# Two soft layers and an attention share their memory, and the turn from dispatch to combination is cut into five stages

## The chip, the cores and the metric

The kernel runs on one core of a Trainium2 chip. The metric is the device time of one execution in microseconds (us). A core has five engines that work at the same time, each from its own queue in order: TensorE (PE in the profile, with PEld for its weight loads), VectorE (DVE), ScalarE (ACT), GpSimd (POOL) and SyncE (SP), which here only issues DMAs; ACT and POOL issue some as well. TensorE writes to PSUM; the other tiles lie in SBUF.

## The reference

The input `x` is 4 x 1024 tokens of width 128, 4,096 tokens in all. Six layers run one after the other, each on a layer norm of `x`: a mixture of experts (MoE), a Mamba layer, the MoE again, a soft mixture of experts ("soft a"), a gated linear attention, and the soft mixture again ("soft b"). The change touches the last three and the constants of the attention.

The soft layer computes `logits = x phi^T + phi_b` for 2,048 slots (64 experts of 32 slots). `D` is its softmax over the 32 slots of an expert; `C` is its softmax over the 64 experts. Then

```
X_tilde = einsum('tznp,tzd->npd', D, x)          # dispatch: 2,048 slot rows
X_tilde = tanh(layernorm(clip(X_tilde)))
Y_tilde = einsum('npd,ndH->npH', X_tilde, expert_w) + expert_b
Y       = einsum('tznp,npH->tzH', C, Y_tilde)    # combination
x       = x + 0.5 * Y
```

The attention has 16 heads of 8. From x it makes q and k (with silu), v, a forget gate f and an output gate g (sigmoids of low-rank products). Its state obeys `S = f * S + k v^T`, its output is `o = q . S`; `o * g` is divided by its root mean square per head, weighted, multiplied by `Wo` and added to x.

## The kernel before

Tokens lie in 32 tiles of 128; `x` stays in SBUF all the time. Inside each layer the order of the instructions on every engine is written out by hand: the program order of the Python code is the queue order.

**Soft layer, `soft_bounded` (L1169).** One loop over k covers two stages. In dispatch, k counts 64 half tiles (128 tokens x 1,024 slots). `logits(k)` makes two products in a PSUM tile of pool `psl` (two buffers), VectorE takes the row's minimum of the negated logits (`nmh`), `expo(k)` exponentiates on ScalarE, `total(k)` sums each expert's 32 slots and inverts on VectorE, `weigh(k)` multiplies on GpSimd, and `spread(k)`, three steps later, adds into the four accumulators `px` in PSUM. From k = 64, u = k - 64 counts 64 units of combination: eight blocks t of 512 tokens, eight pairs c of slot chunks. `clogits(u)` makes two transposed logits tiles, `cexpo(u)` exponentiates them into `L` (pool `lp`, 14 buffers) and adds them on GpSimd into `acc`; after the eighth pair a GpSimd addition folds `acc` to one tile. `denom(t)`, at u = 8t + 9, sums `acc` over the partitions on TensorE (`pd`, L1364) and VectorE inverts it (`rd`). `cweigh(u)` ten units later multiplies L by `rd` on VectorE, `mix(u)` twelve units later multiplies by `yt` on TensorE into `py`. `finish(t)` transposes and adds into x, then calls `after`, which makes the next layer's norm statistics.

**The turn** lies between: at u = 3 to 8 each of the four quarters of `px` goes through `mid_a` (clip on VectorE, transposes on TensorE, statistics on VectorE, a root by POOL's power), one unit later `mid_b` (tanh on ScalarE, transposes, copy), one unit later `mid_c` (32 small matmuls with the experts' weights, bias into `yt`). `maxima(j0, n)` (L1266) reduces `nmh` to one value a token, transposes it on TensorE, and SP brings it by two DMAs through DRAM to the last row of `xT`, which the combination reads. It is called for tiles 0 to 27 at k = 60 and for tiles 28 to 31 at u = 0. All other PSUM tiles of the soft layer come from one pool `psm` of four buffers.

**Attention, `gla_layer` (L1723).** It opens its own pools, loads its weights by ScalarE's DMA queue, builds constants (`sel`, `spread_w`, `hsel`, `hback`) on GpSimd, VectorE and TensorE, and then runs 32 steps: eight half sequences of 512 tokens, four steps each. A step k holds `spread(k+1)` (v's rows copied over partitions, TensorE), `scan(k)` (VectorE), `times_q(k)` (GpSimd), `times_k(k+1)` (VectorE) and `sums(k-2)` (TensorE). `prologue(u)` makes q, k, v, f, g of a half in four pieces, one a step, in the four steps before the half; `epilogue(u)` normalises and adds into x in five pieces, from two steps after the half.

The three layers follow each other as whole calls: `soft("a")`, `gla_layer`, `ln_root`, `soft("b")`, each with pools of its own that reuse the memory of the one before. Soft b sets the rows from 96 on of its `xT` to 1 on GpSimd (L1193) and computes `smod` again. All of this is inside a branch on a flag that bounds the logits; the other branch uses `soft_layer`.

**Second MoE, `moe_experts(..., "b")`.** 16 blocks on TensorE; its hook `extra` issues one piece a block, here the loads of the soft layers' expert weights on ScalarE's queue (`arrive`).

Of the kernel before, what the change touches and what calls it, by code (L numbers as in the profile page):

```python
# [18 lines left out]
P = 128  # L19
# [52 lines left out]
def macaron_kernel(ctx: ExitStack, tc: tile.TileContext, a: dict, out: bass.AP):  # L72
# [1096 lines left out]
    def soft_bounded(phiN, phiM, pbc, ew, eb, tag, ln, first=None, rest=None, after=None, last=False):  # L1169
# [12 lines left out]
        with ExitStack() as s:  # L1182
            sp = s.enter_context(tc.tile_pool(name=f"soft{tag}", bufs=1))
            xnp = s.enter_context(tc.tile_pool(name=f"sxn{tag}", bufs=3))
            ep = s.enter_context(tc.tile_pool(name=f"sep{tag}", bufs=3))
            dp = s.enter_context(tc.tile_pool(name=f"sdp{tag}", bufs=4))
            lp = s.enter_context(tc.tile_pool(name=f"slp{tag}", bufs=14))
            wk = s.enter_context(tc.tile_pool(name=f"swk{tag}", bufs=4))
            psl = s.enter_context(tc.tile_pool(name=f"spl{tag}", bufs=2, space=PSUM))
            psm = s.enter_context(tc.tile_pool(name=f"spm{tag}", bufs=4, space=PSUM))  # L1190

            xT = sp.tile([P, T], F32, name="xT")
            (nc.vector if first else nc.gpsimd).memset(xT[96:P, :], 1.0)  # L1193
            yt = sp.tile([P, NSC, D], F32, name="yt")

            nmh = sp.tile([P, NT, 2], F32, name="nmh")
            nm = sp.tile([P, NT], F32, name="nm")
            nm_d = dram.tile([1, T], F32, name=f"nm_d{tag}")
            smod = group_sum(sp)


            xns, pts, ls, exs, sms, dms, px = {}, {}, {}, {}, {}, {}, {}

            def norm(j):
                g, i = divmod(j, 4)
                if i == 0:
                    xns[g] = xnp.tile([P, 4, D], F32, name="xn")
                ln_apply(xns[g][:, i, :], j, ln)

            def turn(g):  # L1210
                pts[g] = psl.tile([P, HS], F32, name="pt", tag="l")
                for i in range(4):
                    nc.tensor.transpose(
                        pts[g][:, i * P : (i + 1) * P], xns[g][:, i, :], ident
                    )
# [37 lines left out]
            def spread(k):  # L1253
                j, hf = divmod(k, 2)
                dmf = dms.pop(k).rearrange("p n s -> p (n s)")
                for q in range(2):
                    if j == 0:
                        px[hf * 2 + q] = psm.tile([P, 512], F32, name="px", tag="m")
# [881 lines left out]
```

## Time and profile before

| | |
|---|---|
| three executions | 2184.3, 2188.48, 2188.88 us, median 2188.48 |
| profiled execution | 2190.58 us, its span 2188.8 us |
| mean granted TensorE clock | 0.933 |
| second MoE's matmuls | 849 to 971 us of the span |
| soft a, dispatch | 993.5 (first logits) to 1235.7 |
| soft a, combination | 1237.1 (first `clogits`) to 1502 (last update of x) |
| attention, scans | 1516.2 to 1672.6 |
| soft b, dispatch | 1691.8 (first logits) to 1922.4 |
| soft b, combination | 1923.7 to 2184.9 |

Times in the profile count from the start of the span. A line of the timeline begins with start and duration, then engine, source line, operation, output<-input and shapes; a bracket at its end gives how long the engine had been idle before it and what ended that idle time. A float32 product of 128 x 128 by 128 x 512 appears as two MATMUL records; four records in a row are one `clogits`, half a `logits` step with `spread`, or one `mix`. Records of matmuls overlap, so that the distance between their weight loads is the better measure of pace.

### The profile page before, as it was taken

To read this page: it belongs to the slowest core of one execution; us is meant where nothing else is said; L and a number is where in the kernel's file an instruction comes from. 1 tells how busy PE (TensorE), PEld (TensorE's weight loads), DVE (VectorE), ACT (ScalarE), POOL (GpSimd) and SP (SyncE) were. 2 spreads that over 40 slices of the span, in tenths; PEclk is the share of its full clock that TensorE was granted. 3 is DMA by queue.
4 is the path that set the end of the run, shared out by engine and by line. 5 is a ranking of instruction groups with operands and counts; after the bars stand their busy time and mean duration, and the time that the engine had idled before them with its cause. 6 is when DMAs were issued, how large, how long until landed. Compare 5 with 4: busy or idle time off the path is not lost. (4 is left out here: it accounts for less than half of the span.)

```text
span 2188.8 us, 17956 instructions
## 1 busy us (share of the span) xinstructions
PE 1895.3 (87%) x5893; PEld 882.4 (40%) x5893; DVE 1408.3 (64%) x1840; ACT 949.5 (43%) x1593; POOL 1388.7 (63%) x897
## 2 busy tenths in 40 slices
PE   5798488888989866977999899998888999989998
PEld 3465223333333324752444344443233344434443
DVE  6221579878788883126889655556976888744445
ACT  4232465667766523323444333333542333343331
POOL 2677378888988956516886566662533555556663
PEclk9998789999999886998999999998977999999999
DMA  6211522323332321520000000000000000000000
GB/s 233 87 51 49 158 89 97 120 103 101 126 106 99 120 93 50 142 72 25 19 19 7 1 1 0 1 0 6 0 0 1 1 0 0 1 1 6 10 10 16
DMA packets 65117, 110.70 MB, mean 51 GB/s; under 512 B 8159, under 2 KB 41583, under 8 KB 60149
## 3 DMA queue, kind: packets, MB, share of 16 engines
q1 hardware_dynamic: 53990, 87.10, 11.8%
q0 software_dynamic: 8192, 16.79, 2.9%
q10 hardware_dynamic: 2834, 5.59, 0.9%
q8 instruction: 48, 0.79, 0.1%
q14 instruction: 53, 0.43, 0.1%
HBM read 90.00 MB, written 19.44 MB: 50 GB/s over the span
## 5 line engine op out<-in xcount | busy, mean ns | idle before, releaser
L1248 POOL TENSOR_TENSOR dm<-ex,sm 128x1024 f32<-128x1024 f32 x128 | 246.4, 1926 | 166.1 <-DVE sm L1244 95.4
L980 POOL TENSOR_TENSOR hc<-hst,Cs 128x1024 f32<-128x1024 f32 x127 | 281.1, 2222 | 57.2 <-DVE hst L963 33.0
L1356 POOL TENSOR_TENSOR acc<-acc,L 128x1024 f32<-128x1024 f32 x96 | 225.8, 2353 | 113.5 <-ACT L L1348 112.8
L995 PE MATMUL py<-hc,ident 128*128 128x512 f32 x512 | 273.6, 663 | 27.3 <-POOL hc L980 27.1
L1348 ACT ACTIVATE L<-pl,pbc 128x512 f32<-128x512 f32 x256 | 161.9, 683 | 281.1 <-PE pl L1338 270.6
L1236 ACT ACTIVATE ex<-l,nmh 128x1024 f32<-128x1024 f32 x128 | 142.7, 1115 | 293.4 <-DVE nmh L1231 290.8
L1227 PE MATMUL l<-phiT,xT 128*128 128x512 f32 x512 | 248.6, 610 | 12.3 <-ACT ex L1236 9.1
L1259 PE MATMUL px<-dm,xn 128*128 128x512 f32 x512 | 243.3, 598 | 2.5 <-POOL dm L1248 2.2
L1338 PE MATMUL pl<-xT,phiM 128*128 128x512 f32 x512 | 242.8, 599 | 0.0
L1382 PE MATMUL py<-L,yt 128*128 128x512 f32 x512 | 238.4, 593 | 4.4 <-DVE L L1372 4.4
L1231 DVE TENSOR_REDUCE nmh<-l 128x1 f32<-128x1024 f32 x128 | 155.4, 1214 | 76.4 <-PE l L1227 76.0
L953 ACT ACTIVATE dA<-delta,A 128x512 f32<-128x512 f32 x256 | 177.3, 720 | 50.9 <-DVE hst L963 46.2
L945 POOL TENSOR_TENSOR dBu<-du,Bs 128x1024 f32<-128x1024 f32 x78 | 171.4, 2198 | 6.5 <-ACT dA L953 5.4
L450 ACT ACTIVATE hT<-ph,cols 128x512 f32<-128x512 f32 x128 | 87.9, 687 | 190.7 <-PE ph L446 186.3
L995 PEld LDWEIGHTS py<-hc,ident 128*128 128x128 f32 x512 | 94.1, 198 | 171.5 <-issue 115.8
L963 DVE TENSOR_TENSOR_SCAN hst<-dA,carry,dBu 128x512 f32<-128x512 f32 x128 | 155.3, 1262 | 11.8 <-ACT dA L953 6.3
L963 DVE TENSOR_TENSOR_SCAN hst<-dA,dBu 128x512 f32<-128x512 f32 x128 | 147.4, 1202 | 16.9 <-POOL dBu L945 8.5
L1227 PEld LDWEIGHTS l<-phiT,xT 128*128 128x128 f32 x512 | 98.1, 195 | 145.4 <-issue 115.6
L1243 DVE TENSOR_REDUCE sm<-ex 128x32 f32<-128x1024 f32 x128 | 154.5, 1207 | 0.0
L465 DVE TENSOR_TENSOR eo<-po,b 128x512 f32<-128x512 f32 x32 | 22.1, 691 | 196.3 <-PE po L460 188.7
L1382 PEld LDWEIGHTS py<-L,yt 128*128 128x128 f32 x512 | 96.8, 190 | 127.3 <-issue 117.0
L1372 DVE TENSOR_TENSOR L<-L,rd 128x1024 f32<-128x1024 f32 x128 | 147.0, 1210 | 0.1
(292 smaller groups left out, 2967.9 us busy)
## 6 DMA issues: line engine op xcount, KB each, us to landing
Cs<-bc_d SPq DMA_DIRECT2D x32, 1024.0 KB, 6.1
Bs<-bc_d SPq DMA_DIRECT2D x78, 256.0 KB, 3.0
w<-in_w SPq DMA_DIRECT2D x4, 2048.0 KB
y_d<-zero SPq DMA_DIRECT2D x1, 4096.0 KB
y<-y_d SPq DMA_DIRECT2D x16, 256.0 KB, 4.2
ys_d<-eo SPq DMA_DIRECT2D x16, 256.0 KB
ew<-in_ew ACTq DMA_DIRECT2D x12, 320.0 KB, 3.1
x<-in_x SPq DMA_DIRECT2D x8, 256.0 KB, 5.7
```

The costliest lines, as they stand in the source:

```text
L945: eng.tensor_tensor(dBu, r["du"], r.pop(("B", n)).unsqueeze(2).to_broadcast([P, HB, NC]), ALU.mult,)
L953: nc.scalar.activation(dA, r["delta"][:, :, c], AF.Exp, scale=A[:, c * DS + n : c * DS + n + 1],)
L963: nc.vector.tensor_tensor_scan(hst[:, :, c], r.pop(("dA", n, c)), dBu[:, :, c], 0.0 if h == 0 else carry[b][:, c, n : n + 1], ALU.mult, AL ...
L980: eng.tensor_tensor(hc, r.pop(("h", n)), Cs.unsqueeze(2).to_broadcast([P, HB, NC]), ALU.mult)
L995: nc.tensor.matmul(r["py"][:, c, :], ident, hc[:, :, c], start=False, stop=(n == DS - 1))
L1227: nc.tensor.matmul(l[:, q * 512 : (q + 1) * 512], xT[:, j * P : (j + 1) * P], phiN[:, o : o + 512], start=True, stop=True,)
L1248: nc.gpsimd.tensor_tensor(dms[k], exs.pop(k), sms.pop(k).unsqueeze(2).to_broadcast([P, NG, PS]), ALU.mult,)
L1259: nc.tensor.matmul(px[hf * 2 + q], xns[j // 4][:, j % 4, :], dmf[:, q * 512 : (q + 1) * 512], start=(j == 0), stop=(j == NT - 1),)
L1338: nc.tensor.matmul(pl[:, i, :], phiM[:, (2 * c + i) * P : (2 * c + i + 1) * P], xT[:, t * TB : (t + 1) * TB], start=True, stop=True,)
L1348: nc.scalar.activation(L[:, i, :], pl[:, i, :], AF.Exp, bias=pbc[:, 2 * c + i : 2 * c + i + 1], scale=-1.0,)
L1356: nc.gpsimd.tensor_tensor(accs[t], accs[t], L, ALU.add)
L1382: nc.tensor.matmul(pys[t], yt[:, 2 * c + i, :], L[:, i, :], start=(c + i == 0), stop=(c == CS - 1 and i == 1),)
```

## The change

1. **The turn.** `mid_a` and `mid_b` are each split: clip; transposes and statistics; tanh; transposes and copy; experts' matmuls. The five stages stand one unit apart, so the turn takes u = 3 to 10.
2. **Maxima.** `maxima` becomes a generator of two parts: the reduction, and a step later the transpose, the copy and the DMAs. The first call's parts stand at k = 59 and 60, the second's at u = 10 and 11.
3. **Last block's sums.** For t = 7 GpSimd adds only the pairs 0 to 6 and folds; TensorE adds the last pair's two tiles itself in `pd`. The reciprocal is then done in two halves, each followed by the weighing of half of the block's first L; `cweigh` of that unit is dropped.
4. **Shared memory.** `soft_shared` opens `xT`, `nmh`, `nm`, the pools `sxn`, `sep`, `slp`, and PSUM `psl` (two), `psA` (two), `psB` (two) once for soft a, attention and soft b. The attention keeps q, k, v, f, g, the transposed input and the low-rank product of even halves in columns of `xT`, those of odd halves in a small pool of its own; its states and `og` are `L` tiles, its `qs` are `ex` tiles.
5. **Joints.** The attention's first prologue, first `spread` and `times_k` (`begin`) run in the units of soft a after the last `clogits`. Soft a's last `finish` runs at the attention's step 1. Soft b's first norm, turn and two logits (`opening`) run at the attention's steps 30 to 33, and the attention's last epilogue at steps 1 to 4 of soft b's loop. The rows of ones are set in three memsets on GpSimd at steps 28 and 30.
6. **Constants.** The attention's weight loads and constants, and `smod`, are made piece by piece in the second MoE's `extra`, some on VectorE in place of GpSimd.

```diff
+    def soft_shared(s, smod):
...
+        sp = pool("soft", 1)
+        m = SimpleNamespace(
+            xT=sp.tile([P, T], F32, name="xT"),
+            nmh=sp.tile([P, NT, 2], F32, name="nmh"),
+            nm=sp.tile([P, NT], F32, name="nm"),
+            smod=smod,
+            xnp=pool("sxn", 3), ep=pool("sep", 3), lp=pool("slp", 14),
+            psl=pool("spl", 2, space=PSUM),
+            psA=pool("spa", 2, space=PSUM), psB=pool("spb", 2, space=PSUM),
+        )
+        def four(odd, shape, name):
+            return (m.psB if odd % 2 else m.psA).tile(shape, F32, name=name, tag="m")
...
+        def maxima(j0, n):
+            js = slice(j0, j0 + n)
+            nc.vector.tensor_reduce(nm[:, js], nmh[:, js, :], AX.X, ALU.min)
+            yield
+            pt = psl.tile([P, HS], F32, name="pt", tag="l")
+            nc.tensor.transpose(pt[:n, :P], nm[:, js], ident)
...
-            elif c > 1:
+            elif c > 1 and not (t == NB - 1 and c == CS - 1):
                 nc.gpsimd.tensor_tensor(accs[t], accs[t], L, ALU.add)
-            if c == CS - 1:
+            if c == CS - 1 - (t == NB - 1):
...
         def denom(t):
+            pd = m.four(1, [P, TB], "pd")
+            parts = [accs.pop(t)]
+            if t == NB - 1:
+                L = Ls[t * CS + CS - 1]
+                parts += [L[:, 0, :], L[:, 1, :]]
+            for i, part in enumerate(parts):
+                nc.tensor.matmul(
+                    pd, smod.rearrange("p g s -> p (g s)"), part,
+                    start=(i == 0), stop=(i == len(parts) - 1),
+                )
+            rds[t] = m.four(t, [P, TB], "rd")
+            if t < NB - 1:
+                nc.vector.reciprocal(rds[t], pd)
+                return
+            for h in range(2):
+                hs = slice(h * TB // 2, (h + 1) * TB // 2)
+                nc.vector.reciprocal(rds[t][:, hs], pd[:, hs])
+                L = Ls[t * CS]
+                nc.vector.tensor_tensor(
+                    L[:, :, hs], L[:, :, hs],
+                    rds[t][:, hs].unsqueeze(1).to_broadcast([P, 2, TB // 2]), ALU.mult,
+                )
...
+        def opening():
+            for i in range(4):
+                norm(i)
+            yield
+            turn(0)
+            take(0)
+            yield
+            for k in range(2):
+                logits(k)
+                expo(k)
+                yield
...
+            for k in range(NK + CS * NB + XL):
+                next(others, None)
+                if k > 0:
+                    next(before, None)
...
-                        if not new and r == 4:
-                            maxima(0, NT - 4)
-                    if u == 0:
-                        maxima(NT - 4, 4)
+                    if not new and r == 3:
+                        rows = maxima(0, NT - 4)
+                if u == 10:
+                    rows = maxima(NT - 4, 4)
+                if r in (3, 4) and k >= NK - 8 or u in (10, 11):
+                    next(rows, None)
                 if u >= SEAM:
                     v = u - SEAM
-                        for f, o in ((mid_a, 0), (mid_b, 1), (mid_c, 2)):
+                    for f, o in ((mid_a, 0), (mid_a2, 1), (mid_b, 2), (mid_b2, 3), (mid_c, 4)):
...
+                    if u >= CS * NB:
+                        next(tail, None)
...
+        def view(c, n, rows=P):
+            v = m.xT[:rows, c * HB : (c + n) * HB]
+            return v.rearrange("p (i t) -> p i t", t=HB) if n > 1 else v
...
+            qkv = r["qkv"] = own.bp.tile([P, 3, HB], F32, name="qkv") if odd else view(0, 3)
+            fg = r["fg"] = own.bp.tile([P, 2, HB], F32, name="fg") if odd else view(3, 2)
...
+        def begin():
+            yield from prologue(0, lambda name: large(name)[:, 0, :])
+            spread(0)
+            times_k(0)
+            yield
...
+            one.body(tail=begin)
+            run(begin)
+            opening = two.opening()
+            hooks = {k: [lambda: next(opening)] for k in (-2, -1, 0, 1)}
+            hooks[gla.first + 1] = [one.finish]
+            gate = slice(*gla.gates)
+            hooks[-4] = [
+                lambda: nc.gpsimd.memset(m.xT[96:P, : gate.start], 1.0),
+                lambda: nc.gpsimd.memset(m.xT[96:P, gate.stop :], 1.0),
+            ]
+            hooks[-2].append(lambda: nc.gpsimd.memset(m.xT[96:P, gate], 1.0))
+            behind = gla.body(hooks)
+            run(opening)
+            two.body(opened=True, before=behind)
+            two.finish()
```

The hooks' keys count steps from the attention's 32nd: -4 is step 28, 1 is step 33.

## The prediction

> **What bounds the kernel now.** I read the page's busy shares, then the span cut into stretches at the joints between layers, then the instructions in order of time around each joint. A stretch's columns are its length, the busy time of PE, PEld, DVE, ACT and POOL (with counts), the granted TensorE clock, DMA share and GB/s.
>
> ```profile
> PE 1895.3 (87%) x5893; PEld 882.4 (40%) x5893; DVE 1408.3 (64%) x1840; ACT 949.5 (43%) x1593; POOL 1388.7 (63%) x897
> ...
> 1237.00:1287.00 50.00, 42.16 (x226) 20.68 (x226) 21.79 (x56) 20.88 (x41) 29.15 (x16) 0.93 0.00 1
> ...
> 1300.00:1470.00 170.00, 170.00 (x416) 76.43 (x415) 97.78 (x117) 62.95 (x100) 110.22 (x54) 1.00 0.00 0
> 1470.00:1500.00 30.00, 25.22 (x60) 10.27 (x58) 20.96 (x25) 2.19 (x4) 6.47 (x7) 1.00 0.00 1
> 1500.00:1516.00 16.00, 11.28 (x36) 4.58 (x36) 4.48 (x17) 10.18 (x19) 3.27 (x10) 0.79 0.07 19
> 1516.00:1672.00 156.00, 136.96 (x501) 44.11 (x503) 131.46 (x140) 70.41 (x109) 74.55 (x32) 0.85 0.00 1
> ```
>
> In a running soft layer TensorE never pauses (170.00 of 170): a step is eight matmuls started 0.43 us apart, 3.43 us. The attention (1516 to 1672) is VectorE's, 131 of 156 us. The change leaves these steady steps alone and works at the joints: dispatch to combination, 51.8 us in layer a (last dispatch matmul ends 1235.70, first `mix` 1287.49) and 50.4 us in b (1922.38 to 1972.74); soft a to attention; attention to soft b; the end.
>
> **1. The turn in five stages, the last maxima later.** Now each stage puts TensorE behind an engine it has just asked:
>
> ```profile
> 1270.45 1.52 PE L1313 MATMUL pt<-ident,th 128*128 128x128 f32 x4 [1.71 <-ACT th L1307]
> ...
> 1277.63 2.34 POOL L1356 TENSOR_TENSOR acc<-acc,L 128x1024 f32<-128x1024 f32 x1 [5.09 <-ACT L L1348]
> ```
>
> TensorE waits for the tanh, the next `clogits` starts late, and POOL's sums starve behind it. TensorE's own work in that joint: 3 `spread` and 13 `clogits` of 1.72 (27.5), eight groups of transposes of 0.43 (3.4), four `mid_c` of 1.08 (4.3), `pd` 0.86, the maxima's transpose 0.1: 36.2 us of the 51.8. With five stages I walked it unit by unit. The first back transposes (u=6, TensorE there at 1252.5) still meet a tanh that ends at 1254.5, because POOL's root (1.02) now queues behind a sum (2.35): 2.2 us; the next one 0.7; a further 0.7 by u=9: 3.6. The maxima at u=11 occupy one of the two `psl` buffers, so the next `clogits` waits one exponential: 1.3. 36.2 + 3.6 + 1.3 = 41.1, a gain of **10.7**; for b 50.4 - 41.1 = **9.3**. The removed wait for `nm` at u=0 (1.23 us) is in these. The two DMAs of the late rows go to SP's empty queue 11 units later and are needed at u=56, over 140 us on; layer b's first output store is issued at u=21, behind them. Bounds for both layers: 10 (POOL's chain keeps half) to 30 (no stall).
>
> The earlier call, `maxima(0, 28)`, now makes TensorE wait 1.53 us and takes a `psl` buffer: steps 60 to 61 start 5.23 us apart in place of 3.43, 1.8 lost. Reduced a step earlier, only the buffer remains (exponential ends 4.4 after its logits start): 1.0 lost. Gain 0.8 twice, **1.6**.
>
> **2. Soft a to attention.** The attention's first product waits for a prologue begun only after `finish`:
>
> ```profile
> 1514.92 1.23 DVE L1844 TENSOR_TENSOR pv<-pv,qkv 128x1024 f32<-128x1024 f32 x1 [9.45 <-PE pv L1838]
> ```
>
> After: from 1472.66 TensorE has twelve `mix` (20.6), the longer `pd` (2.6, acc and two parts), `po` 0.4 and the prologue: transposes 0.4, q, k, v 2.6, `p1` 0.9, `p2` and the first `pv` 2.8. That is 30.3, so 1503; 2 us of waits for VectorE's weighing: 1505. `pv`(1) then ends at 1506.3, its product at 1507.5, scan(1) at 1510. `finish` now stands in VectorE's queue before scan(2), and POOL, DVE and ACT all have it in order: `times_k`(2) 1.2, x 0.7, four statistics pairs 1.8, eps 0.2, wait for POOL's root 1.1, minus 0.2: scan(2) at 1515.2 in place of 1523.23. Scan(4) today waits 1.35 for `fg`, which would be early: +1. Gain **9**; 4 if the prologue lies wholly on TensorE's queue, 13 if `finish` falls into VectorE's waits.
>
> **3. Attention to soft b.**
>
> ```profile
> 1687.60 3.51 POOL L1193 MEMSET xT<- 32x4096 f32 x1 [12.53 <-PE py L1911]
> 1688.45 2.74 DVE L1166 COPY smod<-sm 128x128 f32<-128x128 f32 x1
> 1691.14 0.59 ACT L1218 COPY xT<-pt 127x512 f32<-127x512 f32 x1 [8.21 <-POOL xT L1193]
> ```
>
> Today everything of soft b waits for the attention's last `py`, then for a memset. After, memset pieces, norm, turn and two logits stand inside the last four attention steps, and epilogue(7) inside dispatch. From the last scan's end (1672.55) in the new order: `pr`(6), turn, sums(30), `py`(6), logits(0), sums(31), logits(1), `nmh`(1), `og`(7), square, root with its table load, reciprocal, and only then total(0) and the first weighing. The clock decides how long that is:
>
> ```profile
> 1656.00:1668.00 12.00, 11.78 (x33) 3.83 (x32) 9.79 (x10) 0.00 (x0) 4.70 (x2) 0.54 0.00 0
> ...
> 1692.00:1697.00 5.00, 5.00 (x6) 1.96 (x7) 1.41 (x2) 1.17 (x2) 0.00 (x0) 0.50 0.00 0
> ```
>
> At 0.50 of the clock logits take 3.4 each: logits(0) ends 1683.8, logits(1) about 1687.5, `og` 1689, reciprocal 1693, weighing 1696.8, logits(4) at 1702.8. Today logits(4) starts 1711.30: gain 8.5. [...] I stay near the row: **10**, of range 4 to 16.
>
> Extra table loads (Exp before the root, Exp after it) are 1.28 us each in this trace, one on the chain and counted. POOL's memsets (3,072 and 1,024 columns, 3.5 us by the row above) run beside scans. The row of `smod` shows a VectorE copy held by a POOL memset (2.74 in place of 0.22); scans beside POOL's product keep 2.33, so I cost nothing, at most 3.5.
>
> **4. The end, sums by TensorE.**
>
> ```profile
> 2160.97 0.30 PEld L1364 LDWEIGHTS pd<-acc,smod 128*128 128x128 f32 x2 [2.58 <-POOL acc L1360]
> ...
> 2166.67 5.42 PE L1382 MATMUL py<-L,yt 128*128 128x512 f32 x12 [1.14 <-DVE L L1372]
> ```
>
> After, `pd` starts at 2159.1 instead of 2160.97 but is 2.6 long: VectorE may start at 2161.9, as now (2162.1). Then it does two half reciprocals (1.7) and two half weighings (0.6) before `cweigh`(55), which `mix`(55) needs: 2166.5 + 1.2 = 2167.7 against 2166.67. **Loss 1.2**; everything after is TensorE's. Between -1 and +2.
>
> **5. Attention's constants in the second MoE.** That stage is TensorE's (15.00 of 15 in its stretches); six transposes, 0.56 + 0.60 by today's rows, lie bare. Four weight loads on ACT's queue (1.9 us to issue) and POOL's small masks lie under `output` (3.4 us of TensorE) and beside gathers with four blocks of lead. **Loss 1.5**, up to 3.
>
> **Sum.** 10.7 + 9.3 + 1.6 + 9 + 10 - 1.2 - 1.5 = 37.9. The profiled execution took 2190.58 (span 2188.8 and 1.8 around it), 2.1 above the median of 2188.48. 2188.48 - 37.9 = **2150.6, forecast 2150**.
>
> **Rivals.**
> [...]
> - *POOL holds the turn*: half the gain there, 10 in place of 20: 2160. For: seven sums and four roots are 21 us of POOL in the joint. Against: POOL is idle 21 of the 50 us now, waiting for exponentials that come late.
> - *Order full at the attention*: joints 2 and 3 give 4 each: 2162.
> - *Slower: shared memory means shared waits.* The attention's q, k, v, f, g of even halves now lie in columns of soft's `xT`. If a write to one column range waits for readers of another, each of 28 prologue pieces puts scan 2.4, `times_q` 2.35, table load 1.3, two activations 1.2 and hops 0.4 in a row: 7.6 against a step's 4.9, +2.7 each, 76: 2226. It decides from 1.4 us a piece. Against it: ranges are kept apart today, ACT writes columns 512 to 1023 and TensorE reads 256 to 383 just after, without a wait for that write:
>
> ```profile
> 1711.15 0.58 ACT L1218 COPY xT<-pt 127x512 f32<-127x512 f32 x1
> ...
> 1711.30 1.98 PE L1227 MATMUL l<-phiT,xT 128*128 128x512 f32 x4 [0.15 <-ACT ex L1236]
> ```
>
> **How the numbers follow.** Forecast 0.57 (its own range 2140 to 2160), everything overlaps 0.12, POOL 0.12, order full 0.08, shared waits 0.11. About 0.2% is what a measurement can tell from no change; a mild form of the last falls within it (0.02), leaving slower 0.09, faster 0.89. Range 2128 to 2171: from a little past full overlap to POOL and order full together (2172); it leaves out the slower case and 0.06 at the edges.
>
> **What would show it.** Joints of about 41 us from last dispatch matmul to first `mix`; scan(1) about 39 us after the last `clogits` of layer a starts (1468.66 to 1519.73 today, 51); logits(4) of layer b about 29 us after the last scan (39 today); the last update of x 31.5 us after the last `clogits` starts (2153.91 to 2184.26 today, 30.4); second MoE 1 to 2 us longer; attention steps unchanged. Wrong if attention's steps stretch, if tanh waits at the turn grow with POOL's queue, or if the clock falls in soft b.

## The result, and the profile after

The changed kernel takes 2198.96 us (median of 6, 2193.89 to 2200.2) where the kernel before takes 2188.68 (median of 6): ratio 1.0042, 95% interval 1.0029 to 1.0056. A second comparison, on another chip on which both kernels are some 2% slower, gave 1.0053 (1.0035 to 1.0071). The forecast was 2150 us; the change makes the kernel slower, by about 10 us.

The span of the profiled execution grew from 2188.8 to 2197.4 us. Cut at the same events in both traces, the difference lies here (times in us; scan(k) is the first scan of the attention's step k, and a time "after the last `clogits`" counts from that step's start):

| stretch | before | after | difference |
|---|---|---|---|
| start to the last dispatch matmul ahead of the first `clogits`, layer a | 1235.70 | 1233.97 | -1.73 |
| turn a: from there to the first `mix` | 51.79 | 52.14 | +0.35 |
| combination a, first `mix` to last `clogits` | 181.17 | 181.17 | 0 |
| last `clogits` to scan(2) | 54.57 | 55.30 | +0.73 |
| scan(2) to scan(8) | 25.16 | 24.40 | -0.76 |
| scan(8) to the end of the last scan | 124.15 | 134.19 | +10.04 |
| from there to the first dispatch matmul of b | 31.23 | 27.14 | -4.09 |
| dispatch b | 218.61 | 216.79 | -1.82 |
| turn b | 50.36 | 53.02 | +2.66 |
| combination b, first `mix` to last `clogits` | 181.17 | 181.17 | 0 |
| last `clogits` to the last update of x | 30.35 | 33.41 | +3.06 |
| sum, to the last update of x | 2184.26 | 2192.70 | +8.44 |

The turns gained nothing, the way into the attention nothing, the attention itself lost 10. Line numbers from here on are those of the kernel that the sentence ahead of the fence names. First the changed kernel's page and two stretches, that of its attention and the one behind it (columns as in the prediction):

```profile
PE 1918.0 (87%) x5901; PEld 896.6 (41%) x5901; DVE 1421.6 (65%) x1848; ACT 951.5 (43%) x1595; POOL 1381.2 (63%) x891
...
1546.98:1681.17 134.19, 120.17 (x412) 41.16 (x412) 103.17 (x117) 53.78 (x85) 59.33 (x27) 0.77 0.00 0
1681.17:1708.31 27.14, 19.38 (x70) 10.38 (x69) 12.26 (x17) 9.08 (x14) 4.26 (x2) 0.71 0.00 1
```

The same stretch, scan(8) to the end of the last scan, in the kernel before:

```profile
1548.39:1672.54 124.15, 109.87 (x412) 36.80 (x412) 102.20 (x113) 53.82 (x84) 55.74 (x24) 0.84 0.00 1
```

TensorE has the same 412 records in both, VectorE and ScalarE nearly the same busy time; GpSimd has three records more, the memsets (3.6 us). What differs on TensorE is the granted clock, 0.77 against 0.84, and with it its busy time, 120.17 us against 109.87.

The timeline of the changed kernel at the turn of layer a shows why nothing was won there:

```profile
1249.89 1.02 POOL L1319 TENSOR_TENSOR srs<-srs,half_t 128x4 f32<-128x4 f32 x1
1250.88 2.34 POOL L1381 TENSOR_TENSOR acc<-acc,L 128x1024 f32<-128x1024 f32 x1
1250.94 2.30 DVE L1321 SCALAR_TENSOR_TENSOR snr<-smv,srs 128x4 f32<-128x4 f32 x1 [1.13 <-POOL srs L1319]
1253.16 0.68 DVE L1300 TENSOR_SCALAR xs<-px 128x512 f32<-128x512 f32 x1
1253.27 1.50 ACT L1327 ACTIVATE th<-pt,snr,srs 128x128 f32<-128x128 f32 x4 [3.83 <-DVE snr L1321]
1253.89 1.11 PE L1311 MATMUL pt<-ident,xs 128*128 128x128 f32 x4 [3.59 <-DVE xs L1300]
```

GpSimd ends the root and starts its next sum. In the same moment VectorE starts `snr`, four numbers a partition, and ends when the sum ends. Behind `snr` wait the tanh on ScalarE, and `xs` on VectorE and with it TensorE. The row of all eight `snr` of both layers, out of the groups of the kernel before and of the changed one:

```profile
L1301 DVE SCALAR_TENSOR_TENSOR snr<-smv,srs 128x4 f32<-128x4 f32 x8 | 1.3, 163 | 9.0 <-POOL srs L1299 9.0
```

```profile
L1321 DVE SCALAR_TENSOR_TENSOR snr<-smv,srs 128x4 f32<-128x4 f32 x8 | 14.1, 1765 | 9.0 <-POOL srs L1319 9.0
```

The mean went from 163 to 1,765 ns: six of the eight took 2.30 us, and in each layer the last took 0.16, where no sum ran. Three tanhs in a row begin 5.86 us apart (1253.27, 1259.12, 1264.98) where a unit of combination needs some 3.4.

### The profile page after: what moved, and what is told of

It is laid out like the page before. It is cut to its first block, busy times and chain, and to the rows that moved or that the text cites. A ratio compares the mean times of both kernels' runs of the same rounds, so it can differ in the third digit from the quotient of the medians.

```text
span 2197.4 us, 17941 instructions
## 1 busy us (share of the span) xinstructions
PE 1918.0 (87%) x5901; PEld 896.6 (41%) x5901; DVE 1421.6 (65%) x1848; ACT 951.5 (43%) x1595; POOL 1381.2 (63%) x891
## 4 chain that ended last, share of the span: by engine, by line
PE 47%; DVE 9%; POOL 3%; ACT 2%; issue 1%; DMA 0%; POOLq 0%; ACTq 0%; DVEq 0%
PE py L1426 10%; PE pl L1363 10%; PE l L1240 8%; PE px L1272 7%; PE ph L446 3%; PE po L460 3%; DVE nmh L1244 2%; PE pv L1954 2%; PE po L1993 1%; DVE sm L1256 1%; POOL dm L1261 1%; ACT ex L1249 1%; PE pq L1928 1%; PE pd L1395 1%; DVE st L1971 1%
## 5 line engine op out<-in xcount | busy, mean ns | idle before, releaser
L995 PE MATMUL py<-hc,ident 128*128 128x512 f32 x512 | 279.6, 677 | 21.2 <-POOL hc L980 21.1
L1381 POOL TENSOR_TENSOR acc<-acc,L 128x1024 f32<-128x1024 f32 x94 | 221.1, 2352 | 102.8 <-ACT L L1373 91.7
L1426 PE MATMUL py<-L,yt 128*128 128x512 f32 x512 | 243.7, 603 | 6.9 <-DVE L L1416 6.9
L1363 PE MATMUL pl<-xT,phiM 128*128 128x512 f32 x512 | 247.4, 607 | 0.8 <-ACT L L1373 0.8
L953 ACT ACTIVATE dA<-delta,A 128x512 f32<-128x512 f32 x256 | 177.3, 720 | 51.1 <-DVE hst L963 46.4
L1272 PEld LDWEIGHTS px<-dm,xn 128*128 128x128 f32 x512 | 96.1, 192 | 120.5 <-issue 110.1
```

The source lines that it names most:

```text
L953: nc.scalar.activation(dA, r["delta"][:, :, c], AF.Exp, scale=A[:, c * DS + n : c * DS + n + 1],)
L995: nc.tensor.matmul(r["py"][:, c, :], ident, hc[:, :, c], start=False, stop=(n == DS - 1))
L1272: nc.tensor.matmul(px[hf * 2 + q], xns[j // 4][:, j % 4, :], dmf[:, q * 512 : (q + 1) * 512], start=(j == 0), stop=(j == NT - 1),)
L1363: nc.tensor.matmul(pl[:, i, :], phiM[:, (2 * c + i) * P : (2 * c + i + 1) * P], xT[:, t * TB : (t + 1) * TB], start=True, stop=True,)
L1381: nc.gpsimd.tensor_tensor(accs[t], accs[t], L, ALU.add)
L1426: nc.tensor.matmul(pys[t], own.yt[:, 2 * c + i, :], L[:, i, :], start=(c + i == 0), stop=(c == CS - 1 and i == 1),)
```

## The experiments

Experiments 1 to 12 ran on one chip, 13 to 16 on another; on both the kernel before takes 2231 to 2234 us. Ratios are to that, with their 95% intervals. Expectations in microseconds were written for the chip of the first result, so a kernel is held against the changed one by the difference of their ratios (1.0053 for the changed kernel on the first of these chips; 0.001 is 2.2 us). Stretches are those of one profiled execution. Some expectations quote a stretch from scan(8) to the end of the last scan that begins a step early: 137.7 (changed kernel, second profile), 129.8 (`e7`), "130 to 133". Counted from scan(8) these are 133.97, 124.37, and 130.70, 134.57, 130.07, 126.47 for the first to the fourth experiment.

### 1. The product of the turn on GpSimd

```diff
+nr = r["nr"] = own.wk.tile([P, 4], F32, name="snr")
+nc.vector.tensor_scalar(nr, mv[:, :, 0], -1.0, None, ALU.mult)
 nc.gpsimd.tensor_tensor(rs, rs, half_t.to_broadcast([P, 4]), ALU.pow)
-nr = r["nr"] = own.wk.tile([P, 4], F32, name="snr")
-nc.vector.scalar_tensor_tensor(nr, mv[:, :, 0], -1.0, rs, ALU.mult, ALU.mult)
+nc.gpsimd.tensor_tensor(nr, nr, rs, ALU.mult)
```

> Base: the changed kernel (2199.0). At the turn from dispatch to combination the product -mean*root (snr, 128x4) goes from VectorE to GpSimd, right behind the root; VectorE only negates the mean before it. In the changed kernel snr took 1.77 us on average (8 of them; 2.30 in six) instead of 0.16, always when GpSimd's next sum (2.35) had started just before it; the tanhs came 5.86 us apart, and the joint from last dispatch matmul to first mix took 52.1 us in layer a (1233.97 to 1286.1) in place of the 41 predicted. Theory A (VectorE and GpSimd hold each other up on their operands in memory): with snr away from VectorE the tanhs come 3.5 to 4.3 us apart, the joints shrink to 41 to 45 us, the kernel is 14 to 22 us faster than the changed one: 2177 to 2185. Rival B (GpSimd's own queue, a root behind each 2.35 us sum, holds the turn): the joints stay at 48 to 52, gain 0 to 6: 2193 to 2199.

Measured: turns of 42.70 and 42.72 us (theory A: 41 to 45), kernel 0.9894 (0.9878 to 0.9911). The timeline of this kernel at the turn of layer a:

```profile
1297.87 1.02 POOL L1321 TENSOR_TENSOR srs<-srs,half_t 128x4 f32<-128x4 f32 x1
...
1298.96 0.20 POOL L1322 TENSOR_TENSOR snr<-snr,srs 128x4 f32<-128x4 f32 x1
...
1299.11 2.35 POOL L1382 TENSOR_TENSOR acc<-acc,L 128x1024 f32<-128x1024 f32 x1
...
1299.20 1.51 ACT L1328 ACTIVATE th<-pt,snr,srs 128x128 f32<-128x128 f32 x4 [1.04 <-POOL snr L1322]
```

The product costs GpSimd 0.20 us, the tanhs are 3.70 us apart (1295.50, 1299.20, 1302.90). GpSimd's sums are as long and as many as before, so its queue (rival B) is not what held the turn. The hold-up that theory A supposes is shown (that it comes of the operands' place in memory is not), and five stages do deliver what they promise once it is gone. The kernel is 35 us ahead of the changed one, more than A's 14 to 22; the rest lies outside of the edit's stage. Its profile has 4.2 us of it between the last `clogits` and scan(2), at a clock of 0.97 in place of 0.88, and 3.5 in the attention, at 0.80 in place of 0.77; the instructions there are unchanged. Its other executions are 8 us faster than the profiled one, and where is not to be seen.

### 2. One fixed order over the three layers

```diff
-            one.body(tail=begin)
+            with tc.manual_schedule(engines=ENGINES):
+                one.body(tail=begin)
...
-                with tc.manual_schedule(engines=ENGINES):
+                with nullcontext():
```

(the second hunk in both bodies)

> Base: the changed kernel. Soft layer a, attention and soft layer b are put under one fixed order, so that the order of the instructions on each engine is that in which the program names them; before, they were three fixed orders, and the compiled VectorE queue has scan(0) and block 6's statistics ahead of the last four weighings cweigh(60) to (63). Theory A (the order at the boundary holds the last mixes back): TensorE's wait of 3.64 us ahead of mix(60) shrinks to under 1.5, scan(2) comes 3 to 7 us earlier after the last clogits of layer a (55.3 us now, 1467.28 to 1522.58), time 2192 to 2196. Rival B (finish and its statistics hold scan(2), wherever scan(0) stands): scan(2) within 1.5 us of now, time 2197 to 2201.

Measured: scan(2) 46.39 us after the last `clogits` in place of 55.30, `scan(0)` now behind `cweigh(63)`. TensorE's wait ahead of `mix(60)` fell from 3.64 to 1.71 us (theory A: under 1.5), and the sixteen records took 7.13 us in place of 10.03, for which the granted clock was 0.71. In the changed kernel VectorE scans ahead of the four weighings (L1416) that TensorE waits for:

```profile
1492.22 1.21 DVE L1971 TENSOR_TENSOR_SCAN st<-xT,pv 128x512 f32<-128x512 f32 x1
...
1498.44 4.61 DVE L1416 TENSOR_TENSOR L<-L,rd 128x1024 f32<-128x1024 f32 x4
...
1499.71 10.03 PE L1426 MATMUL py<-L,yt 128*128 128x512 f32 x16 [3.64 <-DVE L L1416]
```

and here:

```profile
1544.59 4.61 DVE L1416 TENSOR_TENSOR L<-L,rd 128x1024 f32<-128x1024 f32 x4
...
1545.86 7.13 PE L1426 MATMUL py<-L,yt 128*128 128x512 f32 x16 [1.71 <-DVE L L1416]
...
1549.11 2.32 DVE L1971 TENSOR_TENSOR_SCAN st<-xT,pv 128x512 f32<-128x512 f32 x2
```

So theory A holds for the boundary, with more than its 3 to 7 us: the three separately fixed orders had been merged so that scan(0) went ahead of the last weighings. The order is not all of the 8.9 us gained, since the clock in that stretch rose from 0.88 to 1.00, and experiment 1, with the order as it was, had scan(2) 4.2 us earlier at a higher clock. Of the gain, 6.0 us were lost again in the steps just behind: scan(2) to scan(8) took 30.43 us here, 24.40 in the changed kernel. The time was 1.0044 (1.0028 to 1.006), 2 us under the changed kernel and not apart from it by these intervals, as the rival had it, though for another reason than the rival's.

### 3. The last block's sums as before

```diff
-elif c > 1 and not (t == NB - 1 and c == CS - 1):
+elif c > 1:
     nc.gpsimd.tensor_tensor(accs[t], accs[t], L, ALU.add)
-if c == CS - 1 - (t == NB - 1):
+if c == CS - 1:
...
+nc.vector.reciprocal(rds[t], pd)
```

(the two added parts of `pd`, the halves and the dropped `cweigh` go as well)

> Base: the changed kernel. The last block's sums go back to GpSimd wholly, with one reciprocal of 512 columns and no halves, in both layers; all else stays. In the changed kernel the last update of x comes 33.4 us after the last clogits starts (30.4 in the kernel before, 31.5 predicted): TensorE waits 2.87 us for VectorE's weighing and its clock then falls, 12 matmuls in 7.12 us in place of 5.42. Theory A (the halves lengthen VectorE's chain, and the longer wait costs the clock): the tail goes back to 30 to 31 us, kernel 2195 to 2197. Rival B (the clock falls there by chance): tail 32 to 34, kernel 2198 to 2201; in layer a, where the next layer's prologue lies between, no theory expects more than 2 us of either sign.

Measured: tail 30.34 us in place of 33.41, kernel 0.9981 (0.9974 to 0.9988). The tail, the changed kernel first:

```profile
2164.44 1.02 PE L1395 MATMUL pd<-acc,smod 128*128 128x512 f32 x2
2165.29 1.88 PE L1395 MATMUL pd<-L,smod 128*128 128x512 f32 x4
2167.01 3.60 PE L1426 MATMUL py<-L,yt 128*128 128x512 f32 x8
2173.48 7.12 PE L1426 MATMUL py<-L,yt 128*128 128x512 f32 x12 [2.87 <-DVE L L1416]
```

and with the old sums:

```profile
2202.15 1.13 PE L1391 MATMUL pd<-acc,smod 128*128 128x512 f32 x2 [1.80 <-POOL acc L1385]
2203.11 3.60 PE L1410 MATMUL py<-L,yt 128*128 128x512 f32 x8
2207.85 5.42 PE L1410 MATMUL py<-L,yt 128*128 128x512 f32 x12 [1.14 <-DVE L L1400]
```

The new sums do remove the wait of 1.80 ahead of `pd`. They put 2.87 in place of 1.14 behind it, and the next twelve records take 7.12 in place of 5.42. For the tail theory A is shown to 0.1 us. The kernel gained 16 us on the changed one, 13 more than that and outside of both theories: in its profile 5.1 of them lie between the last `clogits` and scan(2) and 3.9 in the attention. The edit stands in layer a too, where it lets TensorE reach `mix(60)` 0.7 us earlier; for the rest of the two the clock was again higher, as in experiment 1 (0.97 in place of 0.88, and 0.80 in place of 0.77).

### 4. The attention's sums over the whole array

```diff
-sel=wp.tile([P, 2, 2, NH], F32, name="sel"),
+sel=wp.tile([P, 2, 224], F32, name="sel"),
...
+o = 96 - (i0 + i) * 32
 nc.tensor.matmul(
-    r["po"][(i0 + i) * 32 : (i0 + i + 1) * 32, :],
-    sel[:, p, :, :].rearrange("e r h -> e (r h)"), qs[:, i, :],
-    start=(p == 0), stop=(p == 1),
+    r["po"], sel[:, p, o : o + P], qs[:, i, :],
+    start=(k % NU == 0 and i == 0), stop=(k % NU == NU - 1 and i == NV - 1),
 )
```

> Base: the changed kernel. In the attention every matmul of sums (out 32 partitions of the array, 128x512 f32) gets a zero-padded weight of 128 columns and accumulates over the whole bank; results are the same, the columns streamed too, but four records that overlapped in 1.05 us should take 1.72. From scan(8) to the end of the last scan the changed kernel took 134.1 us (1546.98 to 1681.1), the one before 124.2; the rows show a granted clock of 0.50 in many stretches of 8 us although TensorE was busy 6.1 to 8.0 of 8. Theory A (the clock falls since too little of the array is at work, not since TensorE pauses): the clock stays at 0.9 or more in the attention, the stretch takes 118 to 128 us, kernel 2186 to 2196. Rival B (pauses decide, or nothing in the program does): the clock stays mixed, and the added 0.7 us a step makes it 4 to 20 us slower: 2203 to 2219.

Measured: clock 0.96 in scan(8) to the end, stretch 126.47 us, kernel 1.0018 (1.001 to 1.0027). The same stretch of this kernel:

```profile
1590.78:1717.25 126.47, 114.99 (x411) 47.63 (x412) 102.74 (x117) 53.71 (x85) 59.32 (x27) 0.96 0.00 1
```

TensorE is busy for hardly a larger share of the stretch than in the changed kernel (115.0 of 126.5, or 91%, against 120.2 of 134.2, or 90%), and yet the clock is 0.96 in place of 0.77. Stretch, clock and time (8 us under the changed kernel) fit A, which holds that the share of the array in use counts. The edit does not separate that from pauses, though: the padded sums no longer overlap, and they alone keep TensorE busy for 51.1 us of the stretch in place of 34.1, so they fill pauses too, as the work added in experiments 13 to 16 does. As a cure it is poor: the stretch is still longer than the 124 us of the kernel before.

### 5 and 6. Both kernels again

> The kernel before, unchanged, for a second profile of its attention. In its first profile the stretch from scan(8) to the end of the last scan took 124.2 us at a granted clock of 0.85, in the changed kernel 134.2 at 0.79, in three changed kernels profiled since 130 to 133. Theory A (the clock in the attention varies from execution to execution in every kernel, and 124.2 was a lucky draw): the stretch takes 127 to 134 us here. Rival B (the change itself lengthens the attention by 6 to 10 us): 122 to 126.

> The changed kernel, unchanged, beside the kernel before on the same chip as the other runs of this group. Its joints should repeat within 0.3 us (52.1 and 53.0 at the turns, 33.4 at the end). Theory A (the attention's clock is a draw of the execution, so the 1.0042 of the first comparison holds some of it): ratio 0.998 to 1.004 and scan(8) to the last scan's end 128 to 135 us. Rival B (the change lengthens the attention): ratio 1.003 to 1.006, stretch 132 to 136.

Measured: 124.40 and 133.97 us from scan(8) to the end, on another chip than 124.15 and 134.19. The turns took 50.48 and 53.79 us in the kernel before and 52.23 and 51.40 in the changed one, so that a turn of either kernel moves by up to 3.4 us between executions, and the +2.66 of turn b in the first table is within that. The kernels repeat their own attention block by block (four steps each; the last ends with the last scan):

| kernel | six blocks from scan(8), us |
|---|---|
| before | 19.34, 19.46, 25.13, 22.26, 20.80, 17.16 |
| before, again | 19.35, 19.45, 25.14, 22.29, 20.87, 17.30 |
| changed | 21.16, 26.22, 22.39, 25.13, 22.38, 16.91 |
| changed, again | 21.10, 26.28, 22.39, 25.13, 22.30, 16.77 |

With two profiles of each, "a lucky draw of the execution" falls. What remains is that the change lengthens the attention, by its memory or order (M), or that it starts the same steps at another moment, from which they are granted another clock (P).

### 7 and 8. The edits that helped, together

`e7` is 1 and 3 together. `e8` adds the one order and moves the statistics of blocks 6 and 7 into the attention:

```diff
+def late(j):
+    ln_stats(lns[4], j)
+    ln_pow(lns[4], j)
+    yield
+    ln_minus(lns[4], j)
+    yield
...
+for j, k in ((24, 5), (28, 9)):
+    piece = late(j)
+    for i in range(2):
+        hooks[gla.first + k + i] = [lambda p=piece: next(p)]
```

> Base: the changed kernel, with both edits that helped alone: -mean*root at the turn on GpSimd (joints 42.7 each, 19.7 us less), and the last block's sums as before (tail 30.3, 3.1 us less). Theory A (the two lie in different stages and add): 22.8 us less than the changed kernel run beside it, joints 42.7, tail 30.3. Rival B (the faster turn already took the other's gain): 18 to 20 us less.

> Base: the kernel with -mean*root on GpSimd and the old sums. Added: one fixed order over soft a, attention and soft b, and the statistics of blocks 6 and 7 of layer a made in the attention's steps 5 and 9 instead of ahead of cweigh(60) and of scan(2), with VectorE's part behind GpSimd's root one step later. Theory A (VectorE's queue holds the boundary: the statistics of block 6 take 1.8 us and a wait for GpSimd ahead of cweigh(60), those of block 7 3.8 us ahead of scan(2)): scan(2) comes 41 to 45 us after the last clogits of layer a starts, against 50 to 55 in the kernels with three orders and 46.4 with one order alone; the kernel is 4 to 9 us faster than its base. Rival B (what is won at scan(2) is given back in the attention, whose VectorE does the same work later and whose clock falls earlier): scan(2) as said, but the kernel within 2.5 us of its base.

Measured: `e7` 0.9944 (0.9927 to 0.996), turns 42.71 and 42.69, tail 30.64; its median is 26.0 us below the changed kernel's of the same group. In their own stages the two edits add, 22.8 us as forecast. The whole times do not: alone the edits gained 35 and 16 us, and `e7` is 11 us slower than `e1`, so that most of what those two won outside of their stages was not the edits' own. Its profiled execution (2208.9 us, the others 2217 to 2219) had in the attention the blocks 19.34, 19.52, 25.08, 22.29, 20.91, 17.23: the pattern of the kernel before, 124.37 us, with the shared memory and all of the new order. So rival M falls: neither the memory nor the memsets lengthen a step. It was the fastest of the four executions; where the others lost 8 to 10 us is not to be seen.

`e8`: scan(2) 40.46 us after the last `clogits`, 14 less than in the kernel before, and the kernel at 0.9925 (0.9908 to 0.9941), 4 us below `e7`: theory A's least gain, though the intervals overlap. And scan(8) to the end was 135.45, at a clock of 0.78, 11 us more than in `e7`'s profile: most of what was won at the boundary was given back, as rival B said.

### 9, 10 and 11. The same attention a little later

In the kernel before, copies that write the same again, three or one, ahead of the first prologue's copy:

```diff
+for _ in range(3 if u == 0 else 0):
+    nc.scalar.copy(xT, pt.rearrange("p i q -> p (i q)"))
 nc.scalar.copy(xT, pt.rearrange("p i q -> p (i q)"))
```

and in `e7` three multiplications of a block of x by 1 behind `finish(7)`.

> Base: the kernel before. Three more ScalarE copies of 0.58 us, of the same data to the same place, stand ahead of the first copy of the attention's prologue: the attention does the same work in the same order, some 1.75 us later. Its two profiles, from two chips, agree step by step (scan(8) to the last scan's end 124.2 and 124.4 us), those of the changed kernel are 134.2 and 137.7, with steps that differ only where the granted clock differs. Theory P (where the pattern of TensorE's busy and idle stretches falls against the clock's gate decides, and the kernel before happens to fall well): the stretch becomes 127 to 138 us, and the kernel 4 to 14 us slower than before, of which 1.7 is the delay itself. Rival M (the shared memory or the other order of the changed kernel costs its attention 10 us): the stretch stays at 123 to 126, the kernel 1 to 3 us slower.

> As the kernel with three copies, with one copy: the attention 0.58 us later. Theory P: the stretch from scan(8) to the last scan's end is another one, 122 to 136 us, not the same as with three copies; kernel 0 to 12 us slower than before. Rival M: 123 to 126, kernel 0 to 2 us slower.

> Base: the kernel with -mean*root on GpSimd and the old sums (0.9944 of before, scan(8) to the last scan's end 129.8 us in its profile). Three VectorE multiplications by 1 of 128x512 stand behind finish(7), ahead of scan(2): 1 to 2 us of delay. Theory P: the stretch changes by more than 3 us in either direction, the kernel's time by -6 to +10. Rival M: the stretch stays within 2 us of 129.8, the kernel 1 to 3 us slower than its base: 0.9949 to 0.9958.

Measured: with three copies the first scan comes 2.6 us later after the last `clogits`, scan(8) to the end takes 132.63 us at a clock of 0.80, the kernel 1.0055 (1.0038 to 1.0072). The stretch in `e7`, with all of the new memory and order of the attention, and then in the kernel before with three copies:

```profile
1578.74:1703.11 124.37, 110.14 (x412) 36.83 (x412) 103.08 (x117) 53.90 (x85) 59.39 (x27) 0.84 0.00 1
```

```profile
1585.74:1718.37 132.63, 115.84 (x412) 40.12 (x412) 102.51 (x113) 53.73 (x84) 55.75 (x24) 0.80 0.00 0
```

With one copy it comes 0.3 us later, the stretch takes 127.15 at 0.82, the kernel 1.0021 (1.0012 to 1.003). `e7` with the multiplications (1.3 us together) takes 127.42 at 0.82 for that stretch and 62.05 in place of 53.37 from scan(0) to scan(8), kernel 0.997 (0.9954 to 0.9986). A kernel that does nothing else than start its attention 2.6 us later is 12 us slower (in the profiles, 2.6 ahead of the scans and 8.2 in the stretch), as much as the whole change cost. So what theory P forecasts is shown: the same steps, started elsewhere, are granted another clock and take another time (0.84 and 124.2 us in the kernel before, 0.80 and 132.6 here). In the kernels without work added on TensorE the stretch follows the clock:

| granted clock | scan(8) to the end, us | kernels |
|---|---|---|
| 0.84 | 124.2, 124.4, 124.4 | before, e7, before again |
| 0.82 | 127.1, 127.2, 127.4 | e12 (next experiment), e10, e11 |
| 0.80 | 130.1, 130.7, 132.6 | e3, e1, e9 |
| 0.77 to 0.78 | 134.0, 134.2, 134.6, 135.5 | changed again, changed, e2, e8 |

### 12. The product on GpSimd in the kernel before

The edit of experiment 1, in the three stages of old.

> Base: the kernel before. The same edit of the turn as in the first experiment, in the three stages of old: -mean*root on GpSimd. There snr took 0.16 us each time, since GpSimd's sums came late and no sum ran beside it. Theory A (the hold-up of VectorE by GpSimd is awakened by the five stages only): the joints of 51.8 and 50.4 us shrink by no more than 2 us each; ratio 0.998 to 1.001. Rival B (the root's way through VectorE was the turn's limit before as well): joints of 44 to 48 us, ratio 0.994 to 0.997.

Measured: turns of 52.09 and 50.46 us (51.79 and 50.36 before), ratio 1.0021 (1.0013 to 1.003). The turn gains nothing: `snr` was never held there (0.16 us in all eight), its hold-up came with the five stages. The kernel is 4.7 us slower, where theory A allowed 2.2. Of these, 2.7 are again the attention, 127.12 at 0.82, off its pattern after an edit more than 200 us ahead of it; where the rest lies is not to be seen. Its first scan came 0.4 us later after the last `clogits`, and its six blocks are those of `e10`, with 0.3 us, to within 0.02 us.

### 13 to 16. Work in TensorE's gaps

Theory G says that too little of TensorE's work in the gaps lets the clock fall. Two products that nobody reads are put into the gap of each epilogue: in the kernel before (`e13`), in the kernel of experiment 1 (`e14`; `e15` has four in place of two) and in that of experiment 8 (`e16`). The edit in `e14`:

```diff
-pm = bank("pm")[:, :P]
+pm = bank("pm")
+for i in range(2):
+    nc.tensor.matmul(pm[:, P:], ident, phiN[:, : HB - P], start=True, stop=True)
+pm = pm[:, :P]
```

> Base: the kernel before. In each epilogue of the attention (8 in all) TensorE multiplies twice 128x384 f32 into the columns 128 to 511 of the bank of pm, which nobody reads, while it would wait for the square on ScalarE (1.56 us in the profile); at full clock this is 1.3 us, at half 2.6. Results are the same. Theory G (too little of TensorE's work in the gaps lets the clock fall): granted clock in scan(8) to the end over 0.90 against 0.85, stretch 118 to 123 us against 124.2, ratio 0.996 to 1.000. Rival P (only where the pattern falls matters; any edit of the kernel before lands on a worse place): clock 0.78 to 0.88, stretch 126 to 134, ratio 1.001 to 1.006.

> Base: the changed kernel with -mean*root on GpSimd (0.9894 of before; scan(8) to the end 130.7 us in its profile). The same two fillers in each epilogue of the attention. Theory G: clock over 0.90, stretch 118 to 125, ratio 0.984 to 0.988. Rival P: stretch 126 to 135, ratio 0.988 to 0.994.

> As e14 with four fillers in each epilogue, 2.6 us at full clock, of which some 1.3 no longer fit into the gap. Theory G: clock 0.92 or more, but up to 1.3 us times 8 of new work on TensorE's queue: stretch 120 to 130. Rival P: stretch 130 to 145 and slower than e14 by 3 to 15 us.

> Base: the kernel with -mean*root on GpSimd, old sums, one order and late statistics (0.9925; stretch 135.5 us at its profile). The same two fillers. Theory G: stretch 118 to 127, ratio 0.984 to 0.989. Rival P: stretch 128 to 138, ratio 0.989 to 0.995.

Measured, from scan(8) to the end, and the kernel:

| run | clock | stretch, us | ratio to before |
|---|---|---|---|
| e13 | 0.90 | 122.59 | 0.9982 (0.9965 to 0.9999) |
| e14 | 0.93 | 121.86 | 0.9918 (0.9893 to 0.9943) |
| e15 | 0.93 | 126.77 | 0.9936 (0.9917 to 0.9955) |
| e16 | 0.81 | 131.86 | 0.9884 (0.9865 to 0.9902) |

In three of four the clock is 0.90 or more, as theory G wants, in `e16` it is not. In time it brings little: `e14` missed G's ratio (0.984 to 0.988) and is not ahead of `e1` (0.9894, on the other chip), which has no filler; `e16`'s ratio is within G's, its stretch within rival P's. So the start and the filling both bear on the clock (in the kernel before, 0.84 became 0.80 with three copies and 0.90 with the filler); by which rule it is granted stays open. `e16` and `e1` are the best kernels here, some 1.1% ahead of the kernel before and 1.6% ahead of the change as it was made.

## Why the prediction was wrong

The step that failed by most is step 1: it put VectorE's hold-up by GpSimd at nothing. Next comes a term that no step had, the clock that the attention is granted (0.77, and 0.84 in the kernel before).

**Step 1, the turn (-20.0 forecast, +3.0 in the table; with the first maxima 21.6).** The unit by unit walk gave 41.1 us a joint; with the hold-up removed it is 42.7 in all joints of the five-stage kernels with that edit. The arithmetic was sound to 1.6 us a joint, the duration of one instruction was not. The walk has no term for `snr`, which leaves it at the 0.16 us of the old turn, though it was now to run beside a sum. The rival "POOL holds the turn" named the right engine and the wrong way: not GpSimd's queue but VectorE, held until GpSimd's sum ended. The trace of before showed it: in layer a's running combination the same operation at L145, between the same two GpSimd instructions, took 2.30 us each of six times. This is one of them:

```profile
1354.06 2.35 POOL L1356 TENSOR_TENSOR acc<-acc,L 128x1024 f32<-128x1024 f32 x1
...
1354.12 2.31 DVE L145 SCALAR_TENSOR_TENSOR nmr<-mv,rstd 128x4 f32<-128x4 f32 x1 [1.13 <-POOL rstd L138]
```

There it cost nothing, since TensorE never paused (170.00 of 170). Step 3 even quoted a copy held by a memset (2.74 us in place of 0.22), and passed on because scans beside GpSimd's product are not (2.33). Not all of VectorE's work is held: `xs`, which reads `px` in PSUM, took 0.69 us at 1240.95 in the changed kernel, inside a sum that ran from 1240.57 to 1242.92. The rows of L145 were what spoke against the change.

The first maxima call gave what was forecast: step 60 to 61 went from 5.23 to 4.40 us in both layers, 0.8 each. The late call costs two waits of 0.69 and 0.40 us in layer a, where 1.3 was counted.

**Step 2, soft a to attention (-9 forecast, 0 at scan(8)).** It put scan(2) 46.5 us after the last `clogits`; measured were 55.3, and 46.4 once the order was as written. Step 2 took the order of the program for the order of the queues, where three separately fixed orders had been merged in another way. That the 46.4 meet the forecast is in part luck: they came at a clock of 1.00, and 6.0 us were lost again in the steps just behind. The forecast for scan(1) held (39 said, 37.0 found) and shows that an early first piece says nothing of the next.

**"Attention steps unchanged" (0 forecast, +10.0).** No step of the sum had a term for it. The prediction's own sign of being wrong, that the attention's steps stretch, came true, though not by the shared memory, its reason for a slower kernel. The instructions are unchanged, the clock at which TensorE runs them is not (0.77 in place of 0.84); experiments 7 and 9 to 12 show that a shift is enough. The kernel before lay well, and the forecast took its 124 us for a property of the work.

**Step 3, attention to soft b (-10 forecast, -4.1).** The row called `logits(4)`, at 1711.30, was `logits(5)`. In the kernel before twelve records are the steps 0 to 2, then come 3 and 4:

```profile
1691.78 8.46 PE L1227 MATMUL l<-phiT,xT 128*128 128x512 f32 x12 [2.48 <-ACT xT L1218]
1700.98 1.98 PE L1227 MATMUL l<-phiT,xT 128*128 128x512 f32 x4 [0.75 <-ACT ex L1236]
...
1706.07 1.98 PE L1227 MATMUL l<-phiT,xT 128*128 128x512 f32 x4 [0.32 <-ACT ex L1236]
```

Measured to its true start, `logits(4)` came 33.5 us after the last scan, and 29.1 in the changed kernel, where the walk said 30.3. The walk was right and its starting point 5.2 us too good. The 16 us at the upper end of this step's range, and with them "everything overlaps" and the 2128 of the whole, rest on TensorE at full clock behind the last scan. No run shows such a gain: to `logits(4)` it was 4.4 us, at a clock of 0.73 in the changed kernel and 0.72 in the kernel before.

**Step 4, the end (+1.2 forecast, +3.1; bound +2).** The delay of the weighing was 1.4 us of it, where 1.2 was forecast (its own two times, 2167.7 and 2166.67, give 1.0). The term missing was the clock: after 2.87 us of waiting, twelve records took 1.7 us more, at 0.76 (2173.48 to 2180.60) in place of 1.00.

**Step 5 (+1.5 forecast).** The loss was smaller: from the second MoE's first matmul to soft a's first logits it takes 144.74 us in place of 144.35. That all ahead of turn a is 1.7 us shorter has other causes: the second MoE begins 1.2 us earlier, ahead of anything that the change touches, and dispatch a is 0.9 shorter, 0.8 of it by the first maxima call.

Of 46.3 us between forecast and result (-37.9 and +8.4), the turns are 23 (some 20 the hold-up, 3 the walk), the attention's clock 10, the boundary 9 (its order, and the clock there), step 3 with its misread row 6, the end 2; the stretches up to the two turns gave 3.5 more than said.

## What to carry to other kernels

When an edit lets two engines work at once, take the duration of a small instruction from a place where it already runs in that company, and look in the trace for rows of the same operation whose durations come in two sizes: 0.16 and 2.30 us here. Compare the compiled order of each engine with the written one wherever two separately ordered parts meet. And do not take a stage's time for a constant where TensorE's clock is below 1 (the same steps took 124 us here at 0.84 and 134 at 0.77): shift it by a microsecond and measure again before an edit is credited or blamed.

## What the runs showed of the hardware

- VectorE's 128x4 products of two SBUF operands took 0.16 us alone and 2.30 where a GpSimd sum of 2.34 us had started 0.06 us before, always to the sum's end. An addition with one tile and a constant (`srs`) was held as well: 1.4 to 1.6 us in experiment 1, to the sum's end, in place of 0.17. `xs`, 128x512 out of PSUM, kept its 0.69 inside a sum.
- TensorE was granted 0.77 of its clock with TensorE busy in 90% of a stretch (the changed kernel's attention) and 0.96 with it busy in 91%, when the sums were padded to 128 columns and kept it busy half as long again (51.1 us in place of 34.1, experiment 4). Between these two the busy share did not tell the clock.
- Two pairs of executions on two chips repeated six blocks of the attention to within 0.2 us, and one copy inside the program, with the first scan 0.3 us later, changed them by up to 4.3. Between executions of one kernel there are jumps as well (`e7`: 2208.9, and 2217 to 2219); what makes them no run here shows.
